# Preparing an LSTM's weights in fewer, larger pieces, half an element apart, in elements 3 to 27

## The chip, the cores and the metric

The kernel runs on one core of one Trainium2 chip. A core has five engines that run side by side, each with its own queue that is worked off in order: TensorE (PE, matrix products, with its weight loads listed as PEld), VectorE (DVE), ScalarE (ACT), GpSimd (POOL) and SyncE (SP), which here does little but issue DMAs. An engine that waits for another waits on a semaphore, and everything behind the waiting instruction in its queue waits with it. The metric is the device time of one execution in microseconds (us); lower is better.

## What is computed

Two layers, each a graph attention followed by a sequence mixer, each added to x, on x of 32 elements x 512 nodes x 256 features with an adjacency of 32 x 512 x 512:

```python
x = x + gnn0(layernorm(x), adj, ...)        # 4 heads, edge type 1
x = x + mamba2(layernorm(x), ...)           # chunked state-space block, 8 heads of 64
x = x + gnn1(layernorm(x), adj, ...)        # 1 head, all edges
x = x + lstm(layernorm(x), ...)             # below

# the LSTM: 32 rows, 512 steps, hidden size 256
x_proj = einsum('btd,gd->btg', x, W_ih) + b_ih + b_hh
gates = x_proj[t] + h @ W_hh.T ; i, f, g, o = split(gates, 4)
c = sigmoid(f) * c + sigmoid(i) * tanh(g) ; h = sigmoid(o) * tanh(c)
logits = lstm_out @ W_lin + b_lin ; w = argmax(logits) * lstm_out
result = 2 * lstm_out + prefix_sum(w) * fw_att + suffix_sum(w) * bw_att
```

The LSTM's weights `W_ih` and `W_hh` (each 256 x 1024 as laid out for the kernel), its biases, and the small vectors `W_lin`, `b_lin`, `fw_att` and `bw_att` don't depend on x. They are brought into the form that the recurrence wants (gates reordered, halved for a tanh-only evaluation, the last input row subtracted from the others) before it starts, and this preparation is what the change moves.

## The kernel before, in words

There are two phases. `layers_per_batch` takes the 32 elements one after the other through everything but the LSTM and stores each result to `X3` in device memory. Then `recurrence` runs 512 steps over all elements at once.

**The order in the first phase.** The work of an element is cut into generators: `plain0` (first attention), `after0` (its norm), `mamba_in` and `mamba_dt` (preparing the mixer), `mamba` (the mixer) and `plain1` with `after1` (second attention, ending with the `X3` store, L878 and L879). Each generator yields a position on a common axis on which 1.0 is one element. Five streams are merged by always running the one with the least position (L1015 to L1018), so that at one time the mixer of element b, the second attention of b - 1 and the first attention of b + 2 run beside each other. That gives the order in which instructions are recorded; a list scheduler then orders each engine's queue before the kernel is built, and semaphores are added where an instruction needs what another engine or a DMA makes.

The end of one element and the start of the next, as it matters here: PE forms the mixer's output `po` (L847) and the sum of its squares `psc` (L859); DVE copies it to `ssc` (L861); POOL makes its reciprocal root, with the helper `rstd_of`: one scaling `ve` (L54) and one power `rs` (L56); DVE adds the scaled output to x (L865). Behind L865 in DVE's queue stand the reductions for the next first attention (L446, L448), whose result ACT needs for `rowsa`, and PE for `pca`. POOL also does the additions of bias vectors: `blin` to x (L605), `beta` to the x of b + 2 (L494), and `bias0` to the first attention's output `o` (L593), which DVE needs for L341.

**The weights.** The fifth stream is `recurrence_weights`. It works in pieces, each of three steps with a yield between: DMAs bring raw weights into an SBUF tile, POOL transforms them, a DMA stores the result to the buffer `wr` in device memory. A piece of `wih` (8 of them: 2 halves k of 128 input rows, 4 quarters q of 256 gate columns) loads `rwraw` and a broadcast row `rwoff`, subtracts (L1132), clears two spare columns of the tile `rwt` (L1069) and does four scalings from `rwraw` into `rwt` (L1075). A piece of `whh` (8 too) loads `rwraw` by four DMAs and has one more scaling, a column from `wl` (L1135). All tiles are of pool `rw0` with one buffer per tag: two tags for `rwraw` (by q), one for `rwoff`, one for `rwt`. So a new `rwt` can't be written until the store of the last one (L1140) has read it. Pieces of `wih` with k = 1 store 127 rows, as their last row is the bias; the others store 128.

`begun` copies one column of the x of the element in progress into a tile ahead of its load, so that the load can't be issued before that element is there. The position of this stream is set in one line (L1014): it starts 1.75 elements before the end and all its steps fall within 1.5 elements. `recurrence` loads `wr` in three DMAs (L1283) when the first phase is done.

Of the kernel before, what the change touches and what calls it, by code (L numbers as in the profile page):

```python
# [14 lines left out]
ALU = mybir.AluOpType  # L15
# [4 lines left out]
P = 128  # L20
N = 512
NT = N // P
D = 256
DK = D // P
# [9 lines left out]
GB = 32  # L34
# [41 lines left out]
def layers_per_batch(ctx, tc, c, a, X3, odd=None, wr=None):  # L76
# [6 lines left out]
    nc = tc.nc  # L83
    nb = a.x.shape[0]
# [917 lines left out]
    def each(*parts):  # L1002
        return stream([(b + at, b + until, make, b + n) for b in range(-2, nb + 1) for at, until, make, n in parts])

    streams = [
        each((0.0, 1.0, mamba, 0)),
        each((-0.097, -0.039, mamba_in, 0), (-0.026, 0.192, mamba_dt, 0)),
        each((0.55, 0.857, second, -1), (0.857, 1.52, first, 2)),
        each((1.62, 1.74, after0, 2)),
    ]  # L1010
    if odd is not None:
        rw = ctx.enter_context(tc.tile_pool(name="rw0", bufs=1))
        now = lambda: states[int(min(at))]["x"][:, 0, 0:1]
        streams.append(nb - 1.75 + 1.5 / 64 * n for n, _ in enumerate(recurrence_weights(nc, rw, a, wr, now)))  # L1014
    END = nb + 10  # L1015
    at = [next(t) for t in streams]
    while min(at) < END:
        n = at.index(min(at))  # L1018
        at[n] = next(streams[n], END)

    if odd is not None:
# [12 lines left out]
        for most, n in ((mall0, H0), (mall1, 1)):  # L1034
            pair = wp.tile([4 * n, n], F32, name=f"pair{n}")
# [12 lines left out]
def recurrence_weights(nc, pool, a, wr, now):  # L1048

    Q, J = 4, 64
    W = 4 * J + 2
    nw = DK * Q * W
    n0 = 2 * nw  # L1060
    half = (0.5, 0.5, 0.5, 1.0)
    order = (3, 1, 0, 2)

    def tile_(p, n, tag):
        return pool.tile([p, n], F32, tag=tag, name=tag)

    def ordered(raw, n, s):
        t = tile_(P, W, "rwt")
        nc.gpsimd.memset(t[:n, 4 * J :], 0.0)  # L1069
        halves = t[:n, : 3 * J].rearrange("p (e g j) -> p e g j", e=2, g=3)  # L1070
        for to, g in enumerate(order):
            dst, src = t[:n, 3 * J : 4 * J], raw[:n, g * J : (g + 1) * J]
            if to < 3:
                dst, src = halves[:, :, to, :], src.rearrange("p (e j) -> p e j", e=2)
            nc.gpsimd.tensor_scalar(dst, src, half[g] * s, None, ALU.mult)  # L1075
        return t

    def begun(t, *columns):
        for n in columns or (0,):
            nc.gpsimd.tensor_copy(t[:, n : n + 1], now())  # L1080
        return t

    yield

    wl = begun(tile_(P, 2 * DK, "rwl"), 0, DK)
    for q in range(Q):
        for l in range(2):
            nc.sync.dma_start(
                out=wl[q * 32 : (q + 1) * 32, l * DK : (l + 1) * DK],
                in_=a.wl[q : q + 1, l * J : (l + 1) * J].rearrange("o (k p) -> p (o k)", p=32),  # L1090
            )
    yield
    nc.gpsimd.tensor_tensor(wl[:, :DK], wl[:, DK:], wl[:, :DK], ALU.subtract)
    bl = begun(tile_(P, 2, "rbl"))
    nc.sync.dma_start(out=bl, in_=a.bl.to_broadcast([P, 2]))
    b = [begun(tile_(P, 4 * J, f"rwraw{n}")) for n in range(2)]
    for t, src in zip(b, (a.bih, a.bhh)):
        nc.sync.dma_start(out=t[:Q], in_=src.rearrange("o (q r) -> (o q) r", q=Q))
    yield
    nc.gpsimd.tensor_tensor(bl[:, 0:1], bl[:, 0:1], bl[:, 1:2], ALU.subtract)  # L1100
    nc.gpsimd.tensor_tensor(b[0][:Q], b[0][:Q], b[1][:Q], ALU.add)
    t = ordered(b[0], Q, 1.0)
    yield
    nc.sync.dma_start(out=wr[:, n0 + 2 * J : n0 + 2 * J + 1], in_=bl[:, 0:1])
    last = wr[P - 1 : P, nw - Q * W : nw].rearrange("o (q w) -> (o q) w", q=Q)
    nc.sync.dma_start(out=last, in_=t[:Q])
    yield
    for n, src in enumerate((a.fw, a.bw)):
        t = begun(tile_(P, W, "rwt"))
        for q in range(Q):  # L1110
            nc.sync.dma_start(out=t[q * GB : (q + 1) * GB, :J], in_=src[q : q + 1, :].to_broadcast([GB, J]))
        yield
        nc.gpsimd.tensor_scalar(t[:, :J], t[:, :J], 0.5, None, ALU.mult)
        yield
        nc.sync.dma_start(out=wr[:, n0 + n * J : n0 + (n + 1) * J], in_=t[:, :J])
        yield
    for n, (src, s) in enumerate(((a.wih, 1.0), (a.whh, 0.5))):
        for k in range(DK):
            for q in range(Q):
                raw = begun(tile_(P, 4 * J, f"rwraw{q % 2}"))  # L1120
                cols = slice(q * 4 * J, (q + 1) * 4 * J)
                if n == 0:
                    nc.sync.dma_start(out=raw, in_=src[k * P : (k + 1) * P, cols])
                    off = begun(tile_(P, 4 * J, "rwoff"))
                    nc.sync.dma_start(out=off, in_=src[D - 1 : D, cols].to_broadcast([P, 4 * J]))
                else:
                    for r in range(Q):
                        r0 = r * J + k * 32
                        nc.sync.dma_start(out=raw[r * 32 : (r + 1) * 32], in_=src[r0 : r0 + 32, cols])
                yield  # L1130
                if n == 0:
                    nc.gpsimd.tensor_tensor(raw, raw, off, ALU.subtract)  # L1132
                t = ordered(raw, P, s)
                if n == 1:
                    nc.gpsimd.tensor_scalar(t[:, 4 * J : 4 * J + 1], wl[:, k : k + 1], 0.5, None, ALU.mult)  # L1135
                yield
                o0 = n * nw + (k * Q + q) * W

                r = P - 1 if n == 0 and k == DK - 1 else P
                nc.sync.dma_start(out=wr[:r, o0 : o0 + W], in_=t[:r])  # L1140
                yield


def recurrence(ctx, tc, c, a, X3, wr, out):
# [247 lines left out]
@with_exitstack  # L1392
def kernel(ctx: ExitStack, tc: tile.TileContext, a, out):
    nc = tc.nc
    nb = a.x.shape[0]
    const = ctx.enter_context(tc.tile_pool(name="const", bufs=1))
    dram = ctx.enter_context(tc.tile_pool(name="dram", bufs=1, space=DRAM))
    c = setup_consts(nc, const)
    X3 = dram.tile([N, nb, D], F32, name="X3")
    wr = dram.tile([P, 2 * DK * 4 * 258 + 2 * 64 + 1], F32, name="wr")  # L1400
    odd = const.tile([1, 1], I32, name="odd")
    with ExitStack() as phase:
        layers_per_batch(phase, tc, c, a, X3, odd, wr)
    general = nc.values_load(odd, min_val=0, max_val=1, skip_runtime_bounds_check_because="it is only compared with 0")
    with tc.If(general > 0):
        with ExitStack() as phase:
            layers_per_batch(phase, tc, c, a, X3)
    with ExitStack() as phase:
        recurrence(phase, tc, c, a, X3, wr, out)
# [70 lines left out]
```

## Time and profile before

| what | value |
|---|---|
| median of 3 runs | 4633.89 us (4614.34 to 4634.27) |
| the profiled execution | 4607.25 us |
| its span | 4605.5 us |
| busy, of the span | PE 85%, DVE 73%, ACT 64%, PEld 53%, POOL 28% |
| from one `ssc` (L861) to the next, elements 0 to 29 | 97.5 to 98.5 us |
| from 29 to 30, and from 30 to 31 | 133.7 and 90.9 us |
| first and last POOL scaling of weights (L1075) | 3026.0 and 3208.6 us |
| first DMA of `wr` into the recurrence | 3294.0 us |
| the rest, to the end | 1311 us, with DVE busy 93% of the time in 3305 to 4530 |

The first phase is a steady loop of 97.8 us for each element, in which PE, ACT, DVE and POOL hand work to each other many times, and its last two elements are of a different length. Durations of single instructions below come from the profiled execution, which is shorter than the median of the runs by 27 us. A column named idle gives the time for which an engine stood still just before an instruction, and what ended it.

### The profile page before, as it was taken

Reading aid. Unit: us, or ns where it says so; the run is one execution under the profiler, and the core shown is the slowest. Engines: PE = TensorE matmul, PEld = TensorE weight load, DVE = VectorE, ACT = ScalarE, POOL = GpSimd, SP = SyncE. Lnnn points to the kernel's source line nnn. Section 1 sums busy time; section 2 is a strip of 40 time slices with the busy share of each in tenths; the row PEclk is TensorE's granted clock in tenths of the full one; section 3 lists DMA queues with packets and bytes.
Section 4 is the critical chain, followed back from the end, with each engine's and each line's share of the span. In section 5 each row is a group of like instructions: output and inputs, shape, how many; then the busy total and the mean of one; then the engine's idle time right before and its main releaser. Section 6 shows DMA issues by size and latency. Waiting matters only on the chain. (4 is left out here: it accounts for less than half of the span.)

```text
span 4605.5 us, 116255 instructions
## 1 busy us (share of the span) xinstructions
PE 3910.5 (85%) x46798; PEld 2447.7 (53%) x46798; DVE 3345.0 (73%) x10429; ACT 2957.3 (64%) x6852; POOL 1275.3 (28%) x1371
## 2 busy tenths in 40 slices
PE   6888899988999888999888999867688888888883
PEld 3445554445554455544455544534466666666662
DVE  4676666676666776666766667745599999999997
ACT  4777777777777777777777777755344444444441
POOL 2333433334333334333334333344000000000000
PEclk8999999999999999999999999988899999999997
DMA  3111222121222212221112221221112222222225
GB/s 109 52 62 57 74 65 72 61 63 57 73 70 67 65 59 65 74 71 61 63 56 74 65 72 60 63 65 57 55 36 45 45 45 45 45 45 44 45 41 167
DMA packets 273755, 288.69 MB, mean 63 GB/s; under 512 B 151872, under 2 KB 224536, under 8 KB 271032
## 3 DMA queue, kind: packets, MB, share of 16 engines
q1 hardware_dynamic: 269832, 271.32, 20.8%
q10 hardware_dynamic: 3216, 9.81, 0.7%
q8 instruction: 371, 6.08, 0.6%
q14 instruction: 176, 1.44, 0.1%
q0 software_dynamic: 160, 0.04, 0.0%
HBM read 227.09 MB, written 37.11 MB: 57 GB/s over the span
## 5 line engine op out<-in xcount | busy, mean ns | idle before, releaser
L1267 PE MATMUL pg<-wall,h 128*32 128x96 f32 x16352 | 558.8, 276 | 176.8 <-DVE h L1349 169.3
L1267 PEld LDWEIGHTS pg<-wall,h 128*32 128x32 f32 x16352 | 374.1, 109 | 350.9 <-DVE h L1349 331.9
L1267 PE MATMUL pg<-wall,xTr 128*32 128x96 f32 (+1 forms) x16384 | 549.0, 274 | 0.0
L484 DVE SCALAR_TENSOR_TENSOR w<-w,adjT 128x1024 f32<-128x1024 f32 x256 | 348.5, 1382 | 249.2 <-ACT w L478 249.2
L1267 PEld LDWEIGHTS pg<-wall,xTr 128*32 128x32 f32 x16384 | 447.3, 110 | 5.0 <-issue 0.3
L710 DVE SCALAR_TENSOR_TENSOR acc<-px,convw,acc 128x511 f32<-128x511 f32 (+2 forms) x480 | 351.3, 744 | 84.6 <-ACT acc L705 76.8
L1326 ACT ACTIVATE z<-pg 128x96 f32<-128x96 f32 x512 | 128.7, 251 | 438.9 <-PE pg L1267 438.9
L478 ACT ACTIVATE w<-rb,neg,colsa 128x512 f32<-128x512 f32 x512 | 387.4, 807 | 8.0 <-PE psu L556 4.4
L746 POOL TENSOR_TENSOR ce<-ce,cT 128x384 f32<-128x384 f32 x128 | 185.2, 1476 | 658.6 <-ACT cT L718 654.9
L548 PE MATMUL pav<-w,hb 128*64 128x512 f32 x1024 | 351.8, 613 | 7.7 <-DVE w L484 4.6
L1337 ACT ACTIVATE z<-z 128x32 f32<-128x32 f32 x1024 | 234.7, 229 | 168.7 <-DVE z L1335 101.0
L829 PE MATMUL py<-g,xdt 128*64 128x128 f32 x2048 | 179.8, 315 | 179.2 <-DVE g L765 131.9
L760 ACT ACTIVATE g<-bc,cs 128x128 f32<-128x128 f32 x1024 | 324.4, 389 | 9.9 <-DMA bc<-line 6.6
L689 PE MATMUL px<-mT,win 128*128 128x512 f32 x640 | 305.1, 608 | 0.0
L54 POOL TENSOR_SCALAR ve<-mv 128x4 f32<-128x4 f32 x32 | 6.2, 194 | 1064.4 <-DVE mv L1191 1064.4
L56 POOL TENSOR_TENSOR rs<-ve,mhalf 128x4 f32<-128x4 f32 (+1 forms) x224 | 276.1, 1233 | 18.4
L847 PE MATMUL po<-wc,xh 128*128 128x256 f32 x1024 | 264.9, 404 | 4.6 <-DVE xh L817 2.5
L829 PEld LDWEIGHTS py<-g,xdt 128*64 128x64 f32 x2048 | 137.7, 157 | 236.3 <-DVE g L765 138.9
L1349 DVE STREAM_TRANSPOSE h<-hh 128x32 f32<-128x32 f32 x1024 | 216.4, 211 | 34.9
L689 PE MATMUL pz<-mT,win 128*128 128x512 f32 x512 | 240.4, 602 | 0.0
L962 PE MATMUL pov<-wb,wv 128*128 128x257 f32 x1024 | 236.5, 384 | 2.0 <-DVE wv L484 2.0
L1332 DVE SCALAR_TENSOR_TENSOR ab<-z 128x64 f32<-128x64 f32 x1024 | 226.7, 221 | 15.1 <-ACT z L1326 11.8
(249 smaller groups left out, 8539.6 us busy)
## 6 DMA issues: line engine op xcount, KB each, us to landing
bc<-line SPq DMA_DIRECT2D x128, 512.0 KB, 3.6
adj<-in_adj_dram SPq DMA_DIRECT2D x32, 1024.0 KB
rb<-linea SPq DMA_DIRECT2D x64, 512.0 KB, 5.0
ce<-line SPq DMA_DIRECT2D x64, 384.0 KB, 4.6
x<-in_x_dram SPq DMA_DIRECT2D x32, 512.0 KB, 6.5
X<-x SPq DMA_DIRECT2D x32, 512.0 KB
xt<-X SPq DMA_DIRECT2D x128, 128.0 KB, 2.1
x<-X SPq DMA_DIRECT2D x128, 128.0 KB, 3.5
```

Source lines behind the costliest of these rows:

```text
L56: nc.gpsimd.tensor_tensor(rs, ve, c.mhalf[:, :n], ALU.pow)
L478: nc.scalar.activation(w[:, t, k, :], rb[:, k, :], AF.Relu, bias=neg1, scale=cols[:, 2 * m + t, h + k : h + k + 1],)
L484: nc.vector.scalar_tensor_tensor(w[:, :, k, :], w[:, :, k, :], 1.0, edges, ALU.add, ALU.mult)
L548: nc.tensor.matmul(pa[k * HO : (k + 1) * HO, :], hb[:, j, 2 * q + k, :], w[:, t, k, :], start=(j == 0), stop=(j == NT - 1),)
L689: nc.tensor.matmul(pz, win[:, k, col : col + P], mT[:, k, :], start=(k == 0), stop=(k == DK - 1))
L710: nc.vector.scalar_tensor_tensor(acc[:, s:], pz[:, : N - s], convw[:, cc, k : k + 1], acc[:, s:], ALU.mult, ALU.add)
L760: nc.scalar.activation(g[:, i, k, :], bc[:, k, i * P : (i + 1) * P], AF.Relu, bias=cs[:, i, 2 * cc + k : 2 * cc + k + 1], scale=-1.0,)
L829: nc.tensor.matmul(py[k * HD : (k + 1) * HD, i * P : (i + 1) * P], xdt[:, i, h * HD : (h + 1) * HD], g[:, i, k, :], start=(i == 0), stop=F ...
L847: nc.tensor.matmul(po[:, i * D : (i + 1) * D], xh[:, cc, it * P : (it + 1) * P], wc[:, cc, :], start=(cc == 0), stop=(cc == NC - 1),)
L962: nc.tensor.matmul(po[:, : D + 1], ws[j // 2][:, j % 2, 0, it * P : (it + 1) * P], wb[:, j, :], start=(j == 0), stop=(j == NT - 1),)
L1267: nc.tensor.matmul(p[q * GB : (q + 1) * GB, :], lhs[k], w[:, k, q, s:e], start=(start and k == 0), stop=(stop and k == DK - 1),)
L1337: nc.scalar.activation(z[:, (10 + n) * H : (11 + n) * H], z2[:, 4 * n * H : (4 * n + 1) * H], AF.Tanh, scale=0.5)
```

## The change

The position of the fifth stream changes: its steps now start at 3.25 and are (32 - 8)/48 = 0.5 elements apart. The work is cut differently:

- `rwraw` and `rwt` have one tag each and are twice as wide. `rwraw` takes raw weights and the broadcast row side by side (in `wih`), or two quarters (in `whh`); `rwt` two quarters.
- `ordered` takes one or two quarters. Three of its four scalings are now two each, of 32 columns for every quarter, so it has seven instead of four.
- `whh` has four pieces of two quarters each instead of eight; `wih` keeps eight of one, in the order q, k instead of k, q.
- `fw` and `bw` share a tile, a scaling and a store; the loads of `wl` come in two steps.

What is computed and stored is the same. The core of the diff:

```diff
-        streams.append(nb - 1.75 + 1.5 / 64 * n for n, _ in enumerate(recurrence_weights(nc, rw, a, wr, now)))
+        streams.append(3.25 + (nb - 8) / 48 * n for n, _ in enumerate(recurrence_weights(nc, rw, a, wr, now)))
...
-    def ordered(raw, n, s):
-        t = tile_(P, W, "rwt")
-        nc.gpsimd.memset(t[:n, 4 * J :], 0.0)
-        halves = t[:n, : 3 * J].rearrange("p (e g j) -> p e g j", e=2, g=3)
+    def ordered(raw, n, quarters, s):
+        t = tile_(P, 2 * W, "rwt")
+        tq = t.rearrange("p (q w) -> p q w", q=2)[:n, :quarters]
+        rq = raw.rearrange("p (q w) -> p q w", q=quarters)[:n]
+        nc.gpsimd.memset(tq[:, :, 4 * J :], 0.0)
         for to, g in enumerate(order):
-            dst, src = t[:n, 3 * J : 4 * J], raw[:n, g * J : (g + 1) * J]
+            src = rq[:, :, g * J : (g + 1) * J]
             if to < 3:
-                dst, src = halves[:, :, to, :], src.rearrange("p (e j) -> p e j", e=2)
-            nc.gpsimd.tensor_scalar(dst, src, half[g] * s, None, ALU.mult)
-        return t
+                for e in range(2):
+                    nc.gpsimd.tensor_scalar(
+                        tq[:, :, (3 * e + to) * 32 : (3 * e + to + 1) * 32], src[:, :, e * 32 : (e + 1) * 32],
+                        half[g] * s, None, ALU.mult,
+                    )
+            else:
+                nc.gpsimd.tensor_scalar(tq[:, :, 3 * J : 4 * J], src, half[g] * s, None, ALU.mult)
+        return t, tq
...
+    t = begun(tile_(P, 2 * W, "rwt"))
     for n, src in enumerate((a.fw, a.bw)):
-        t = begun(tile_(P, W, "rwt"))
         for q in range(Q):
-            nc.sync.dma_start(out=t[q * GB : (q + 1) * GB, :J], in_=src[q : q + 1, :].to_broadcast([GB, J]))
+            nc.sync.dma_start(out=t[q * GB : (q + 1) * GB, n * J : (n + 1) * J], in_=src[q : q + 1, :].to_broadcast([GB, J]))
         yield
-        nc.gpsimd.tensor_scalar(t[:, :J], t[:, :J], 0.5, None, ALU.mult)
-        yield
-        nc.sync.dma_start(out=wr[:, n0 + n * J : n0 + (n + 1) * J], in_=t[:, :J])
-        yield
+    nc.gpsimd.tensor_scalar(t[:, : 2 * J], t[:, : 2 * J], 0.5, None, ALU.mult)
+    yield
+    nc.sync.dma_start(out=wr[:, n0 : n0 + 2 * J], in_=t[:, : 2 * J])
+    yield
...
+    for q in range(Q):
+        cols = slice(q * 4 * J, (q + 1) * 4 * J)
         for k in range(DK):
...
+            pair = begun(tile_(P, 2 * 4 * J, "rwraw"), 0, 4 * J)
+            raw, off = pair[:, : 4 * J], pair[:, 4 * J :]
+            nc.sync.dma_start(out=raw, in_=a.wih[k * P : (k + 1) * P, cols])
+            nc.sync.dma_start(out=off, in_=a.wih[D - 1 : D, cols].to_broadcast([P, 4 * J]))
+            yield
+            nc.gpsimd.tensor_tensor(raw, raw, off, ALU.subtract)
+            t, _ = ordered(raw, P, 1, 1.0)
+            yield
+            o0 = (k * Q + q) * W
+            r = P if k < DK - 1 else P - 1
+            nc.sync.dma_start(out=wr[:r, o0 : o0 + W], in_=t[:r, :W])
+            yield
+    for q in (0, 2):
+        for k in range(DK):
+            raw = begun(tile_(P, 2 * 4 * J, "rwraw"))
+            for r in range(Q):
+                r0 = r * J + k * 32
+                nc.sync.dma_start(out=raw[r * 32 : (r + 1) * 32], in_=a.whh[r0 : r0 + 32, q * 4 * J : (q + 2) * 4 * J])
+            yield
+            t, tq = ordered(raw, P, 2, 0.5)
+            for e in range(2):
+                nc.gpsimd.tensor_scalar(tq[:, e, 4 * J : 4 * J + 1], wl[:, k : k + 1], 0.5, None, ALU.mult)
+            yield
+            o0 = nw + (k * Q + q) * W
+            nc.sync.dma_start(out=wr[:, o0 : o0 + 2 * W], in_=t)
+            yield
```

More of the change, by code (lines that the diff above doesn't have):

```diff
@@ L1085, in recurrence_weights @@
     wl = begun(tile_(P, 2 * DK, "rwl"), 0, DK)
-    for q in range(Q):
-        for l in range(2):
+    for l in range(2):
+        for q in range(Q):
             nc.sync.dma_start(
@@ L1095, in recurrence_weights @@
     nc.sync.dma_start(out=bl, in_=a.bl.to_broadcast([P, 2]))
-    b = [begun(tile_(P, 4 * J, f"rwraw{n}")) for n in range(2)]
+    both = begun(tile_(P, 2 * 4 * J, "rwraw"), 0, 4 * J)
+    b = [both[:, : 4 * J], both[:, 4 * J :]]
     for t, src in zip(b, (a.bih, a.bhh)):
@@ L1101, in recurrence_weights @@
     nc.gpsimd.tensor_tensor(b[0][:Q], b[0][:Q], b[1][:Q], ALU.add)
-    t = ordered(b[0], Q, 1.0)
+    t, _ = ordered(b[0], Q, 1, 1.0)
     yield
@@ L1105, in recurrence_weights @@
     last = wr[P - 1 : P, nw - Q * W : nw].rearrange("o (q w) -> (o q) w", q=Q)
-    nc.sync.dma_start(out=last, in_=t[:Q])
+    nc.sync.dma_start(out=last, in_=t[:Q, :W])
     yield
+    t = begun(tile_(P, 2 * W, "rwt"))
     for n, src in enumerate((a.fw, a.bw)):
-        t = begun(tile_(P, W, "rwt"))
         for q in range(Q):
-            nc.sync.dma_start(out=t[q * GB : (q + 1) * GB, :J], in_=src[q : q + 1, :].to_broadcast([GB, J]))
+            nc.sync.dma_start(out=t[q * GB : (q + 1) * GB, n * J : (n + 1) * J], in_=src[q : q + 1, :].to_broadcast([GB, J]))
@@ L1112, in recurrence_weights @@
         yield
-        nc.gpsimd.tensor_scalar(t[:, :J], t[:, :J], 0.5, None, ALU.mult)
-        yield
-        nc.sync.dma_start(out=wr[:, n0 + n * J : n0 + (n + 1) * J], in_=t[:, :J])
-        yield
-    for n, (src, s) in enumerate(((a.wih, 1.0), (a.whh, 0.5))):
-        for k in range(DK):
[L1119 to L1141, printed above, removed]
@@ new lines, in recurrence_weights @@
+    nc.gpsimd.tensor_scalar(t[:, : 2 * J], t[:, : 2 * J], 0.5, None, ALU.mult)
+    yield
+    nc.sync.dma_start(out=wr[:, n0 : n0 + 2 * J], in_=t[:, : 2 * J])
+    yield
+    for q in range(Q):
+        cols = slice(q * 4 * J, (q + 1) * 4 * J)
+        for k in range(DK):
+            pair = begun(tile_(P, 2 * 4 * J, "rwraw"), 0, 4 * J)
[10 more added lines that the diff above has]
+            yield
@@ new lines, in recurrence_weights @@
+    for q in (0, 2):
[11 more added lines that the diff above has]
+            nc.sync.dma_start(out=wr[:, o0 : o0 + 2 * W], in_=t)
+            yield
```

## The prediction

> **What bounds the kernel now.** I read the page first. Its chain of work that ended last starts only at the recurrence (3291 us to the end), which the change does not touch, so the 3290 us before it must be read by stage. The table of windows compares one steady element, 1640.5 to 1738.3, with elements 30 and 31, each counted from its first `zs` (L697). Columns: us, then busy us of PE, PEld, DVE, ACT, POOL, then granted clock, DMA share, GB/s.
>
> ```profile
> 1640.50:1738.30 97.80, 87.61 (x432) 49.49 (x431) 66.55 (x140) 73.26 (x131) 36.89 (x33) 0.97 0.22 65
> 3031.30:3168.60 137.30, 92.91 (x401) 48.33 (x400) 66.83 (x137) 66.64 (x119) 53.30 (x92) 0.84 0.20 55
> 3168.60:3250.10 81.50, 57.22 (x275) 35.62 (x275) 37.16 (x66) 46.10 (x85) 25.91 (x66) 0.87 0.24 70
> ```
>
> Element 30 has the work of any other and takes 137.3 us instead of 97.8. The waits of 3105 to 3220 (engine, line, releaser: total, times, longest) say why:
>
> ```profile
> DVE o L341 <- POOL o L593: 30.8, 1, 30.8
> POOL rwt L1069 <- DMA wr<-rwt: 27.9, 8, 8.2
> ACT dec L670 <- DMA wr<-rwt: 7.1, 1, 7.1
> ACT g L760 <- DMA bc<-line: 6.6, 2, 4.8
> ```
>
> DVE waits 30.8 us for a bias addition on POOL, and POOL is late because weight pieces stand ahead of it, each waiting until the previous one has left the only `rwt` buffer. The timelines of POOL and SP (start, us, what, idle before and its releaser) show two prices for that wait:
>
> ```profile
> 3087.70 0.25 SPq L1140 DMA_DIRECT2D wr<-rwt  x1
> 3095.85 0.10 POOL L1069 MEMSET rwt<- 128x2 f32 x1 [8.05 <-DMA wr<-rwt]
> 3106.53 0.10 POOL L1069 MEMSET rwt<- 128x2 f32 x1 [8.19 <-DMA wr<-rwt]
> 3106.59 2.48 POOL L593 TENSOR_TENSOR o<-o,bias 128x512 f32<-128x512 f32 x2
> ...
> 3174.83 0.34 SPq L1140 DMA_DIRECT2D wr<-rwt  x1
> 3176.68 0.10 POOL L1069 MEMSET rwt<- 128x2 f32 x1 [1.75 <-DMA wr<-rwt]
> ```
>
> A store of 128 rows frees the buffer 1.85 us after its issue (3174.83 to 3176.68); one of the four with 127 rows takes 8.15 us (3087.70 to 3095.85; the other three 8.1 to 8.2).
>
> Last, a steady element where the moved work will stand, timelines of POOL and DVE:
>
> ```profile
> 1646.57 2.49 POOL L494 TENSOR_TENSOR x<-x,beta 128x512 f32<-128x512 f32 x2
> 1649.02 1.27 POOL L605 TENSOR_TENSOR x<-x,blin 128x512 f32<-128x512 f32 x1
> 1652.61 0.20 POOL L54 TENSOR_SCALAR ve<-ssc 128x4 f32<-128x4 f32 x1 [2.32 <-DVE ssc L861]
> 1652.89 1.02 POOL L56 TENSOR_TENSOR rs<-ve,mhalf 128x4 f32<-128x4 f32 x1
> ...
> 1652.36 0.16 DVE L861 COPY ssc<-psc 128x4 f32<-128x4 f32 x1 [6.88 <-PE psc L859]
> 1653.94 0.48 DVE L865 SCALAR_TENSOR_TENSOR x<-po,rs,x 128x256 f32<-128x256 f32 x1 [1.42 <-POOL rs L56]
> 1654.46 0.68 DVE L446 TENSOR_REDUCE mall<-pra 16x1 f32<-16x512 f32 x1
> ```
>
> POOL has 2.32 us free before L54. But L54 is on the loop that sets the 97.8 us: followed back step by step from one L861 to the one before, each instruction starts within 0.2 us of what releases it: psc (PE), L861, POOL L54 and L56, DVE L865, L446 and the queue behind them as far as `da` (L650), then PE. While POOL is late there, DVE stands at L865, and behind it L446 and L448; ACT's `rowsa` and PE's `pca` (1656.47) wait for those.
>
> **What the Trainium skill says.** "DMA: Bandwidth & Descriptors", section "Why a DMA increments its semaphore by 16 and not by 1", says that the number of engines is the largest up to 16 that divides the slowest dimension, so 128 rows use 16 and 127 rows one. The trace agrees: 127 packets of 1032 B follow one another over 6.7 us, 128 of them are done in 0.5. "TensorE: Matmul & The Clock Gate", section "What's actually happening", has PE fall to half clock after an idle window of about 3.4 us. The trace agrees: 0.50 is granted in 1635.3 to 1642, behind a 4.1 us wait of PE, and in 3109.5 to 3116.5, after the long stall.
>
> **The change, part by part.** The compiled order of the changed kernel keeps every other instruction of SP, POOL, DVE, ACT and PE in its place up to the work of element 31, apart from the moved work.
>
> (1) Elements 30 and 31 lose the work: the gain. Element 30 needs 97.8 at most; three things differ at its end. Its L861 came 125.2 us after its first `zs`, against 88.9 in a steady element; without first(32), whose transposes and `pra` interleave with `po`, I take 86.5. From L861 to the next first `zs` it took 12.2; a `rs` held up by 2 us behind a weight piece goes, leaving 10.2. So 96.7 for 137.3: 40.6 gained. In element 31 three stalls go: ACT's 7.1 (its `line` store waited for the slot of a weight DMA; 6.8 of it passes on), 1.8 and 4.8 for `bc`, which SP issued late behind weight DMAs: 13.4. Together 54. At least 47 (the stalls of 31 half hidden), at most 62 (ACT's new order there helps as well). The last 33.4 us, from L865 of element 31 to the last `X`, stay.
>
> (2) Eight wih pieces, all in one place, at the ends of elements 6 to 17. SP issues `raw` and `off` after the adj load, on POOL's copies, at about 1646.9 and 1647.3 in the element above. `off` was used 3.1 to 3.3 us after issue in the tail, so 1650.5. POOL's second L605 ends at 1650.7 (0.36 later, for two copies). Then the subtraction 0.73 and gap 0.1, six scalings of 128x32 (64 columns start every 0.33, one column every 0.14 to 0.17, so about 0.245) 1.47, and one of 64 columns 0.37: end at 1653.35, 0.75 after L54 is due. That alone would be small. But the next piece's memset stands right behind, **ahead of L54**, and waits until this piece's store has left the buffer; with one `rwt` the stall that cost most before comes along.
>  - 128 rows (k = 0): store at 1653.4, memset at 1655.5 (1.85, and 0.25 for traffic), L54 at 1655.6: 3.0 late. Bounds 2.0 and 4.5.
>  - 127 rows (k = 1): store at 1653.4, memset at 1661.55, L54 at 1661.65: 9.0 late. Bounds 8.3 and 11.
>
>  Four of each: 12 + 36 = 48. Nothing hides it, as L54 is on the loop.
>
> (3) PE idles meanwhile from 1656.45 and comes back at half clock. After the long stall of element 30, the stretch from the first xdt (L783) to the last `came` (L812) took 10.0 us for a steady 7.7: 2.3. I take 2.3 for each 9 us stall and 1.2 for each 3 us one: 14. Bounds 0 and 20.
>
> (4) Four whh pieces, at the ends of elements 18 to 23, stand behind L56 of L54's pair. Six scalings of 64 columns 2.0 and one of 128 about 0.5 from 1653.9 end at 1656.4; store of twice the bytes 2.4, memset and two one-column scalings 0.6: the next L54 (1658.40) starts at 1659.6, 1.2 late. Three times, since no memset follows the last: 3.6. Bounds 0 and 10.
>
> (5) The beginning: bias block about 0.6; the eight `wl` loads hold SP 4 us, so x lands near 1655, and its statistics start at 1658.2: nothing. fw and bw: one scaling of 0.5 ends before 1652.6: nothing, and its memset falls in the 4.5 us before the next L54. The last wih piece carries 0.5 more. Together 1.1.
>
> (6) Moved past on SP: `X` out goes 2.3 us later (nobody waits), the x load behind the store's wait 5 us later, landing by 1658 (k = 0) or behind the slow store by 1664, where its statistics start at 1661 or 1667: nothing, with 3 us to spare.
>
> Sum: −54 + 48 + 14 + 3.6 + 1.1 = +13 us. The profiled execution took 4607.25 (span 4605.5), so 4620. The median shown is 4633.89, 27 above it; 13 on top gives 4647. About 23 us, 0.5%, is what a measurement of this kernel can tell from no change.
>
> **Rivals.**
> A, the stalls come to more. In the 127-row pieces the store's engine also carries x rows, and PE's lost clock adds where PE is the tight one; or element 31 keeps its stalls. At 13 us for each k = 1 piece and 7 for each k = 0, 80 is lost with (4) and (5) at 5 more; against 54 that is +31, 4665. It decides once the eight pieces cost 73 together, the mean then over 9. For it: nothing is free behind L54. Against: store and load times are measured.
> B, faster: the stall is absorbed. Were the store or the loop looser than I read it (another buffer of the pool given to the next `rwt`, or stages that make up half of it), 20 would be lost and 54 gained: −34, 4600. It decides below 31 us lost. For it: POOL is busy 28% overall. Against: no gap over 0.2 us on that loop, and the memset's wait stands in the compiled order.
> C, the change does not do what it says, the tail keeping its stalls: excluded for POOL and SP, since nothing of it is left there; that 30 and 31 shrink by under 35 for another reason gives +32 and goes with A.
>
> **How the numbers follow.** My case has 52 in 100, A with C 36, B 12. The gain's 47 to 62 and the losses' ends (piece stalls 41 to 62, clock 0 to 20, whh 0 to 10) span −20 to +46 if all ends fall together. A leans upward, so I keep the upper end and take −16 to +46 for 8 in 10: 4618 to 4680. Faster by over 0.5%: B, 0.12. Within: 0.52. Slower: 0.36.
>
> **What would show it.** From one L861 to the next: about 95 us from element 29 to 30 instead of 133.7, and about 76 from 30 to 31 instead of 90.9; behind elements 6 to 17, alternately about 102 and 109, with 97.8 between; the wait of memset `rwt` for `wr<-rwt` still some 40 us, and POOL's `rs` as what DVE L865 waits for. Part (2) is wrong if L54 starts within 1 us of L861 there, part (3) if the granted clock stays 1 behind the stalls, part (1) if DVE still waits on L593 by tens of us.

## The result, and the profile after

The changed kernel takes 4638.9 us (median of 20 runs, 4621.0 to 4646.2); the kernel before, run beside it, 4618.7 us (20 runs, 4603.7 to 4639.3). The ratio is 1.0031, with a 95% interval of 1.0016 to 1.0045: about 14 us slower (7 to 21), which on the 4633.9 us shown before is 4648. It is not the quotient of the medians, which lie 20 us apart: the runs of before fall into two groups, eleven from 4604 to 4619 us and nine from 4633 to 4639, and their median is at the edge of the lower one. The means, 4637.4 and 4623.2, differ by 14. The profiled executions differ by more, 4605.5 to 4634.8 us of span, in large part because a steady element takes 97.9 us on average in the one of before, and 98.9 in many elements without a piece in that of the changed kernel. Both lengths come without any difference of work (last section).

First the windows, for the same columns as before: an element that follows a piece of 127 rows (from its L861 to the next), one that follows a piece of 128 rows, one without a piece, and then elements 30 and 31, each from its first `zs`.

```profile
976.40:1085.20 108.80, 90.08 (x430) 50.38 (x431) 66.58 (x140) 73.15 (x130) 39.77 (x44) 0.92 0.20 63
1085.20:1187.70 102.50, 89.96 (x431) 50.38 (x430) 66.58 (x140) 73.17 (x130) 38.19 (x38) 0.95 0.23 69
1187.70:1286.60 98.90, 88.74 (x431) 49.34 (x431) 66.51 (x140) 73.24 (x130) 37.60 (x35) 0.97 0.20 62
...
3112.10:3213.20 101.10, 88.23 (x402) 47.39 (x400) 65.51 (x137) 67.10 (x122) 30.89 (x28) 0.97 0.13 42
3213.20:3280.70 67.50, 54.53 (x276) 35.21 (x275) 37.36 (x65) 45.31 (x83) 12.89 (x12) 0.94 0.18 56
```

DVE, ACT and POOL are as busy in the first three windows as in any other element; the extra 10 and 4 us are waiting. Elements 30 and 31 went from 137.3 and 81.5 to 101.1 and 67.5: the tail's gain is there, and the loop has given it back, and more.

Where, the waits over the whole span show (total, times, longest), first of before, then of after:

```profile
POOL rwt L1069 <- DMA wr<-rwt: 48.7, 13, 8.2
DVE x L865 <- POOL rs L56: 44.0, 31, 1.4
```

```profile
DVE x L865 <- POOL rs L56: 99.1, 32, 11.7
POOL rwt L1072 <- DMA wr<-rwt: 50.0, 12, 8.3
```

POOL waits for its own stores as long as before, 50 us. What changed is who stands behind it: DVE's wait for `rs` at L865, 1.4 us in every element before, has grown by 55 us. One piece of each kind in the timelines of POOL, SP and DVE of the changed kernel:

```profile
977.24 0.37 POOL L1082 TENSOR_SCALAR rwt<-rwraw 128x64 f32<-128x64 f32 x1
985.82 0.10 POOL L1072 MEMSET rwt<- 128x2 f32 x1 [8.22 <-DMA wr<-rwt]
986.00 0.20 POOL L54 TENSOR_SCALAR ve<-ssc 128x4 f32<-128x4 f32 x1
...
977.63 0.25 SPq L1140 DMA_DIRECT2D wr<-rwt  x1
977.98 1.09 SPq L108 DMA_DIRECT2D x<-in_x_dram  x1
...
976.41 0.16 DVE L861 COPY ssc<-psc 128x4 f32<-128x4 f32 x1 [6.61 <-PE psc L859]
987.35 0.48 DVE L865 SCALAR_TENSOR_TENSOR x<-po,rs,x 128x256 f32<-128x256 f32 x1 [10.78 <-POOL rs L56]
...
1709.67 0.10 POOL L1072 MEMSET rwt<- 128x2 f32 x1 [2.08 <-DMA wr<-rwt]
```

The scalings are done at 977.61, 1.2 us after `ssc`. Then the memset for the next piece, an element or more away, waits 8.22 us for the store of this one, and L54 behind it comes 9.6 us after L861; behind the 128-row piece (1709.67) the wait is 2.08.

From one L861 to the next: 102.5 to 102.6 us behind the four pieces of 128 rows, 108.8 to 109.5 behind the four of 127, and 98.4 to 99.2 in nearly all others up to element 22. From element 0 to 29 that is 2921.2 us against 2838.3 before (+82.9), from 29 to 31 174.3 against 224.6 (-50.3).

### The profile page after: what moved, and what is told of

Its sections match the earlier page's. It is cut to its first block, busy times and chain, and to the rows that moved or that the text cites. A ratio compares the mean times of both kernels' runs of the same rounds, so it can differ in the third digit from the quotient of the medians.

```text
span 4634.8 us, 116234 instructions
## 1 busy us (share of the span) xinstructions
PE 3936.6 (85%) x46798; PEld 2457.6 (53%) x46798; DVE 3345.3 (72%) x10429; ACT 2954.4 (64%) x6852; POOL 1276.3 (28%) x1384
## 5 line engine op out<-in xcount | busy, mean ns | idle before, releaser
L484 DVE SCALAR_TENSOR_TENSOR w<-w,adjT 128x1024 f32<-128x1024 f32 x256 | 347.8, 1379 | 248.1 <-ACT w L478 248.1
L710 DVE SCALAR_TENSOR_TENSOR acc<-px,convw,acc 128x511 f32<-128x511 f32 (+2 forms) x480 | 351.5, 743 | 75.6 <-ACT acc L705 67.8
L746 POOL TENSOR_TENSOR ce<-ce,cT 128x384 f32<-128x384 f32 x128 | 185.1, 1475 | 696.0 <-ACT cT L718 679.0
L829 PE MATMUL py<-g,xdt 128*64 128x128 f32 x2048 | 167.9, 299 | 178.8 <-DVE g L765 131.7
L54 POOL TENSOR_SCALAR ve<-mv 128x4 f32<-128x4 f32 x32 | 6.2, 193 | 1063.9 <-DVE mv L1205 1063.9
L829 PEld LDWEIGHTS py<-g,xdt 128*64 128x64 f32 x2048 | 125.8, 145 | 240.8 <-DVE g L765 138.9
L689 PE MATMUL pz<-mT,win 128*128 128x512 f32 x512 | 253.1, 629 | 0.0
```

The costliest lines, as they stand in the source:

```text
L484: nc.vector.scalar_tensor_tensor(w[:, :, k, :], w[:, :, k, :], 1.0, edges, ALU.add, ALU.mult)
L689: nc.tensor.matmul(pz, win[:, k, col : col + P], mT[:, k, :], start=(k == 0), stop=(k == DK - 1))
L710: nc.vector.scalar_tensor_tensor(acc[:, s:], pz[:, : N - s], convw[:, cc, k : k + 1], acc[:, s:], ALU.mult, ALU.add)
L829: nc.tensor.matmul(py[k * HD : (k + 1) * HD, i * P : (i + 1) * P], xdt[:, i, h * HD : (h + 1) * HD], g[:, i, k, :], start=(i == 0), stop=F ...
```

## The experiments

The claims to test: the loss is the memset's wait for the store, at the one place where L54 stands behind it (rival: the block of scalings and its loads); and the tail's loss was the same wait. All ratios are to before, with 95% intervals; the three columns on the right come from the profiles, L861 to L861. Each is one execution, and the two lengths of a steady element alone can move the column 0 to 29 by up to 32 us.

| kernel | median us | ratio | element 0 to 29 | 29 to 30 | 30 to 31 |
|---|---|---|---|---|---|
| before | | 1 | 2838.3 | 133.7 | 90.9 |
| changed | 4638.9 | 1.0031 (1.0016 to 1.0045) | 2921.2 | 100.1 | 74.2 |
| e1_halves | 4631.8 | 1.0028 (1.0012 to 1.0044) | 2915.8 | 99.9 | 75.5 |
| e2_split127 | 4604.9 | 0.9991 (0.9970 to 1.0011) | 2888.6 | 98.7 | 74.2 |
| e3_place | 4575.3 | 0.9909 (0.9878 to 0.9941) | 2857.8 | 99.8 | 75.6 |
| e4_before_split | 4597.2 | 0.9962 (0.9942 to 0.9983) | 2857.4 | 118.3 | 85.1 |
| e5_none | 4589.1 | 0.9917 (0.9888 to 0.9947) | 2838.0 | 100.4 | 73.9 |
| e6_late | 4616.7 | 0.9983 (0.9961 to 1.0004) | 2869.2 | 117.2 | 93.5 |
| e7_two_tiles | 4648.0 | 1.0055 (1.0035 to 1.0075) | 2929.8 | 99.9 | 77.9 |
| e9_place_split | 4555.3 | 0.9888 (0.9843 to 0.9933) | 2838.3 | 100.1 | 74.1 |
| e10_one_memset | 4608.5 | 0.9976 (0.9958 to 0.9995) | 2891.7 | 99.8 | 75.6 |
| e11_spread | 4629.5 | 1.0031 (1.0013 to 1.0049) | 2915.6 | 99.9 | 77.9 |
| e12_both | 4580.9 | 0.9919 (0.9892 to 0.9946) | 2864.5 | 98.7 | 74.2 |

**A second place for the result (e1, e7).** Two ways to give the memset a buffer that is free:

```diff
-            t, _ = ordered(raw, P, 1, 1.0)
+            t, _ = ordered(raw, P, 1, 1.0, pairt[:, k * W : (k + 1) * W])   # e1: halves of one tile
...
-        t = tile_(P, 2 * W, "rwt")
+        t = tile_(P, W, f"rwt{h}")                                         # e7: h = k for wih
```

> The changed kernel with one thing undone: pieces of wih with k = 0 use the left half of the buffer rwt and those with k = 1 the right half, so that the memset that stands ahead of L54 (ve<-ssc) no longer waits for the store just issued. Size, loads, scalings and their places stay. My theory (the wait of the memset is the price): L54 starts about 1 us after L861 behind the pieces instead of 3.5 and 9.9; only the last piece, behind which a memset of the whole buffer stands, still costs some 9. Gain against the changed kernel 4 x 2.5 + 3 x 8.9 = 37 us and up to 10 of lost TensorE clock; against before a ratio of 0.990 to 0.996. Rival (the block itself, its loads or its traffic delay L54): L54 still over 3 us late and the ratio at 1.000 or above.

> The changed kernel with two separate tiles of one quarter each, rwt0 for k = 0 and rwt1 for k = 1, in place of one of two quarters; whh pieces fill both and store them with two DMAs (fourteen scalings for seven, some 1.3 us more in each of four pieces). In seven of the eight wih pieces the memset ahead of L54 then waits for a store of an element or two ago; only behind the last one it still waits for the store just issued. My theory (the wait is the price): L54 starts 1 to 1.5 us after L861 behind the first seven pieces and some 10 behind the last; 4 x 2.4 + 3 x 8.8 = 36 us gained, 5 lost in whh, 31 in all against the changed kernel, ratio against before 0.993 to 0.998. Rival (halves e1 changed nothing since the block itself is the price): L54 late as in the changed kernel and the ratio at 1.001 or above.

Both expectations fail. The memset waits 47.6 us for stores in either kernel, and L54 comes as late as in the changed kernel behind all eight pieces but one of e1. This is not the rival's doing. In the traces the memset stands as early as its data allow: with two buffers the one for the piece after next has come forward too, to just behind the last piece that used its half, and waits for that piece's store as before (it starts 8.1 to 8.2 us after the issue of each 127-row store of e1). One piece of e1 tells the two apart by accident. It has no memset behind it (the next one clears both halves, and must wait for the other):

```profile
1709.33 0.37 POOL L1082 TENSOR_SCALAR rwt<-rwraw 128x64 f32<-128x64 f32 x1
1709.78 0.20 POOL L54 TENSOR_SCALAR ve<-ssc 128x4 f32<-128x4 f32 x1
```

There L54 came 1.29 us after L861: the block alone costs 1.0 us (a steady L54 comes after 0.25). The ratio of e7 is above that of the changed kernel, though the intervals overlap; its longer whh pieces, of fourteen scalings and two stores, go with three elements of 100.4 to 103.9 us.

**The number of rows (e2).**

```diff
-            nc.sync.dma_start(out=wr[:r, o0 : o0 + W], in_=t[:r, :W])
+            for r0, r1 in ((0, r),) if r == P else ((0, 112), (112, r)):
+                nc.sync.dma_start(out=wr[r0:r1, o0 : o0 + W], in_=t[r0:r1, :W])
```

> The changed kernel with the store of 127 rows issued as two, of 112 and of 15 rows, and nothing else. My theory (k = 1 pieces cost three times as much as k = 0 pieces because one DMA engine carries all their 127 rows): L54 starts 3.5 to 4 us after L861 in k = 1 pieces too, instead of 9.9; 4 x 6.2 = 25 us and up to 4 of clock gained against the changed kernel; ratio against before 0.995 to 0.999. Rival (k = 1 pieces are slow for their place or the traffic of x at that time): under 5 us gained, ratio 1.002 or above.

The waits of e2 over the span:

```profile
DVE x L865 <- POOL rs L56: 75.7, 32, 5.6
POOL rwt L1072 <- DMA wr<-rwt: 25.9, 12, 2.4
```

As expected: the longest wait falls from 8.3 to 2.4, L54 comes 3.6 to 4.0 us after L861 behind these pieces too, and their elements take 101.7 to 102.6 us for 108.8 to 109.5. The ratio falls from 1.0031 to 0.9991, just above the range that I expected. The row count is the cause of the difference between the two kinds of piece.

**The memset itself (e10).**

```diff
+    rwt = tile_(P, 2 * W, "rwt")
+    nc.gpsimd.memset(rwt, 0.0)
...
-        nc.gpsimd.memset(tq[:, :, 4 * J :], 0.0)
```

> The changed kernel with one tile rwt for all pieces, whose spare columns are cleared once at the start instead of by a memset in each piece. Still one buffer; but the first instruction of the next piece that writes it is now a scaling, which stands behind that piece's load, an element or two later. The memset was placed as early as its buffer allowed, right behind the last piece that had used it, which is why halves (e1) and two tiles (e7) left its wait where it was. My theory (that wait is the price, not the block): L54 starts about 1.3 us after L861 behind seven pieces, as behind the one piece of e1 that had no memset behind it; behind the last one, where a column of wl takes the memset's place, it still starts about 10 after. Gain 4 x 2.3 + 3 x 8.5 = 35 us against the changed kernel; ratio against before 0.993 to 0.998. Rival (the block of a piece is the price): as the changed kernel, 1.001 or above.

L54 comes as expected: 0.3 to 2.1 us after L861 behind seven pieces, 9.6 behind the last. So the wait is what held it up. The ratio lies in the range too. But three elements behind 127-row pieces still take 105.2 to 106.6 us, although their L54 is about 1 us late. The timelines of SP and DVE, and then the waits over the span, show for e10 what the stall had covered:

```profile
973.38 0.25 SPq L1142 DMA_DIRECT2D wr<-rwt  x1
973.72 1.11 SPq L108 DMA_DIRECT2D x<-in_x_dram  x1
...
983.02 0.43 DVE L65 BATCH_NORM_STATS2 bnst<-x 128x6 f32<-128x256 f32 x1 [3.86 <-DMA x<-in_x_dram]
```

```profile
DVE x L865 <- POOL rs L56: 62.8, 32, 10.8
POOL rwt L1153 <- DMA wr<-rwt: 15.6, 4, 8.3
DVE bnst L65 <- DMA x<-in_x_dram: 15.3, 4, 3.9
```

The load of the next x is issued 0.34 us behind the 127-row store and lands 9.3 us after its issue. DVE waits at L65, and behind L65 stand `ee` (L635) and what leads to `da`. (One wait of 3.7 is at the kernel's start, in every kernel here; three of 3.9 are new.)

**Both (e12).** e10 with e2's split.

> e10 (spare columns cleared once) and the 127-row stores issued as two, of 112 and 15 rows. In e10 L54 came only 0.9 to 1.3 us after L861 behind pieces of k = 1, but these elements still took 105.2 to 106.6 us, and DVE L65 waited 3.9 us for the x load, which SP issues 0.3 us behind the slow store. My theory now (the one-engine store has a second price, the x load that shares its engine; the memset's wait covered it): no wait of L65 for x, k = 1 elements at 98.5 to 100 us but for the last, about 102; 18 to 20 us less than e10, ratio against before 0.989 to 0.996. Rival (something else holds k = 1 elements, such as TensorE's clock after the piece): they stay over 104 us and the ratio within 0.002 of e10's 0.9976.

The waits of e12 over the span:

```profile
DVE x L865 <- POOL rs L56: 58.4, 32, 4.9
DVE bnst L65 <- DMA x<-in_x_dram: 3.7, 1, 3.7
```

No wait of L65 for x is left but that at the start, and the elements behind 127-row pieces take 98.8 to 99.7 us, the last one 102.7. In the first of them L65 reads the x 4.8 us after its issue and need not wait, against 9.3 us with the wait in e10. From 0 to 29 it is 27 us less than e10, where I had expected 18 to 20: 20 us in the three elements whose L65 waited, 6 in the last one, where the wait for the buffer is shorter too (400.8 for 426.8 in the four). The ratio goes from 0.9976 to 0.9919. A 127-row store therefore has two prices, the wait for the buffer and the x load behind it; how it holds that load back is not shown. In the changed kernel the first hides the second.

**The place (e3, e9), and the floor (e5).**

```diff
-        now = lambda: states[int(min(at))]["x"][:, 0, 0:1]
+        now = lambda: da[:, 0, 0:1]
```

> The changed kernel with one thing changed: the column that begun copies ahead of a load comes from da (L650, mid-element) and not from x. The same pieces with the same single buffer and the same waits then stand behind the last statistics of an element on POOL, ahead of L746, where POOL is free for over 20 us. My theory (the same wait costs nothing where nothing on the loop is queued behind it): the memsets of rwt still wait some 40 to 50 us for stores, but L54 (ve<-ssc) starts 0.25 us after L861 in every element; 55 us or more gained against the changed kernel, ratio against before 0.986 to 0.992. Rival (the work costs the loop time wherever it stands, by its traffic, by sharing POOL and DVE, or by the TensorE clock): ratio 0.998 or above, and elements with a piece longer than those without.

> e3_place (begun copies a column of da) and the 127-row stores issued as two, of 112 and 15 rows. My theory (in that place a wait of 8 us has nothing queued behind it that is needed): the waits of memset rwt fall from 52 to some 26 us and the time does not move, ratio within 0.002 of e3's 0.991. Rival (a slow store still costs by its engine or by what it delays on SP): 0.988 or below.

> The preparation of the weights is left out: the buffer wr is filled with zeros by nine DMAs in elements 3 to 8, so the LSTM computes with zero weights; everything else is the changed kernel's. This is the floor for any place of the work. My theory (in e3 the work costs nothing where it stands): within 0.002 of e3's 0.991. Rival (it still costs by traffic or sharing): below 0.988. For the lengths of elements: if stretches of 98.9 to 99.0 us for an element instead of 97.5 to 98.4 come here too, they have nothing to do with the weights.

e5 leaves the preparation out: nine DMAs fill `wr` with zeros in elements 3 to 8, and the LSTM computes with zero weights. The waits of e3 over the span, and its POOL timeline at a 127-row piece:

```profile
POOL rwt L1072 <- DMA wr<-rwt: 51.7, 12, 8.3
DVE x L865 <- POOL rs L56: 45.4, 32, 1.4
```

```profile
998.20 0.10 POOL L1072 MEMSET rwt<- 128x2 f32 x1 [8.27 <-DMA wr<-rwt]
1001.86 5.60 POOL L746 TENSOR_TENSOR ce<-ce,cT 128x384 f32<-128x384 f32 x4 [3.56 <-DMA ce<-line]
```

The same pieces with the same single buffer wait 51.7 us, even longer than in the changed kernel, and L865 no longer feels it: 45.4, its 1.4 us in each element. L54 comes 0.25 us after L861 everywhere. Behind the memset POOL waits another 3.6 us for L746's own data. The ratio, 0.9909, is as I expected. e9 halves the memset's waits (27.1); its 0.9888, of six runs, lies between my range and the rival's, and the intervals don't tell it from e3's. Without the preparation (e5) the ratio is 0.9917, as expected, and element 0 to 29 takes 2838.0 us against 2838.3 with it in e9. In that place no cost of the work can be seen, and e3 and e9 beat both kernels by 0.9 to 1.4%.

**The parts alone (e4, e6, e11).** e4 is before with only the split of e2; e6 has the changed kernel's pieces at the position of before; e11 has before's pieces at the changed position:

```diff
-        streams.append(3.25 + (nb - 8) / 48 * n for ...      # changed
+        streams.append(nb - 1.75 + 1.5 / 48 * n for ...      # e6
...
-        streams.append(nb - 1.75 + 1.5 / 64 * n for ...      # before
+        streams.append(3.25 + (nb - 8) / 64 * n for ...      # e11
```

> The kernel before with its four stores of 127 rows issued as two each, of 112 and of 15 rows, and nothing else. My theory of the tail (element 30 is 40 us too long since L593 stands behind weight pieces, three of which wait 8.2 us for a 127-row store): these waits fall to about 2 us each; element 30 gets 15 to 25 us shorter, ratio 0.994 to 0.997. Rival (the number of pieces or their loads set element 30's length): element 30 as before, ratio within 0.002 of 1.

> The changed kernel's pieces at the position of before (1.75 elements before the end, all within 1.5 elements): one part of the change alone, the size. My theory (the tail's cost is the waits for the stores, and the four 127-row stores stay): 29 to 30 stays over 120 us, ratio 0.996 to 1.003. Rival (larger pieces are the gain by themselves): ratio below 0.994.

> The kernel before with its own sixteen small pieces, at the changed kernel's place: steps from 3.25, (32 - 8)/64 = 0.375 apart. This is the other part of the change alone, the spreading. My theory (the loss is the memset's wait on the loop, the gain the emptied tail; the size does neither): L54 3 to 4 us late behind four pieces of wih and some 9.8 behind four, nothing behind pieces of whh; 29 to 30 about 100 us; ratio against before 1.000 to 1.005, as the changed kernel's. Rival (fewer and larger pieces are needed for the spreading to pay): 1.008 or above, with whh pieces that delay the loop too.

The waits of e4 in its elements 30 and 31 (3040 to 3260 us):

```profile
POOL rwt L1069 <- DMA wr<-rwt: 24.1, 13, 3.2
DVE o L341 <- POOL o L593: 14.4, 1, 14.4
```

As expected, 29 to 30 falls by 15.4 us by the split alone, from 133.7 to 118.3, as L341's wait for L593 falls from 30.8 to 14.4; 30 to 31 goes from 90.9 to 85.1. So about 21 of the tail's 50 us were the price of the 127-row stores. In e6 29 to 30 is 117.2 (I had written over 120), 30 to 31 is 93.5: larger pieces in the old place shorten the one and not the other, and the interval of the whole holds 1. e11 comes out at the changed kernel's 1.0031, with L54 2.8 to 3.1 us late behind four pieces and 8.7 to 9.3 behind four; pieces of whh delay it by 0.3 to 1.2, which I had put at nothing. So the size of the pieces hardly matters to the loss; the spreading makes it.

## Why the prediction was right

The forecast was 4647 with 13 us lost; measured is 1.0031, 14 us. The mechanism was right: the tail's stalls go, and the memset's wait costs the loop about as much at L54. That the two numbers agree to 1 us is luck. The interval alone is 7 to 21 us; steps 1 and 2 below were 8 us too good together, which step 3 made up with 2 to 11 us too much; and 4633.9, the base, is the median of three runs of which two were of the longer group, while the profile it was joined to is of the shorter. Step by step, against the profile:

1. Tail: 54 expected, 50.3 measured. Element 31 gave 14.0 for 13.4. Element 30 gave 36.2 for 40.6, and the term that was off is the 86.5 us to its L861: I had taken 2.4 off a steady element for the missing first(32), but it took 91.6, and 91.8 with no weights anywhere (e5). From there to the next `zs` 9.5 for 10.2. That "L861 29 to 30" would be about 95 came from the same term; it is 100.1.
2. The eight wih pieces: 48 expected. L54 was late by 3.2 to 3.6 (expected 3.0) and 9.3 to 10.3 (expected 9.0), 13.3 + 38.8 = 52.1 in all. The mechanism is shown by e2, e10 and e3: the rows set its size, the memset carries it, the place decides whether it counts. The "Trainium skill", page "DMA: Bandwidth & Descriptors", section "Why a DMA increments its semaphore by 16 and not by 1", gave the row rule, and 8.2 against 2.2 us for 127 rows and 112 + 15 (e2) agrees.
3. Half clock after the stalls: 14 expected. The clock does fall: 0.50 is granted for 13.7 us behind each 127-row piece and for 6.8 behind each of 128 rows, 0.92 and 0.95 in the mean of the windows above. But its price could not be separated. The loop's 82.9 us less 52.1, the 1.5 by which the bias piece held up L54 and the 4.3 below leave 25 us: 13 of them in the 19 elements that have no piece, many of 98.9 us, and 12 in the eight. e3 has 17 elements of 99.0 us or more without any stall of L54. Measured against 98.9 the eight elements exceed it by 55.5 us, which leaves 3.4 for the clock; against 97.9 it would be between 11 and 12. Step 3 was right in size only if one counts the second way, and the prediction did not know of the two lengths.
4. whh: 3.6 expected, as three times 1.2. The first statistics' L54 was 1.1 late in three elements, 18, 20 and 21. But only one of them, 20, is longer, 103.2 us, 4.3 above the next, with 6.8 us of half clock from 17.7 us behind its L861; 18 and 21 took 98.6 and 98.9. So the sum came near for another reason than the one given, and why 20 alone is longer stays open.
5. Beginning: 1.1 expected, the bias piece alone held up L54 by 1.5.
6. SP: right, as L65 finds the loaded x at 992.52 without a wait, 14.5 us after its issue; with the 9.3 us to landing of e10 some 5 us were to spare, for 3 expected. But I did not say what they hang on. The start at 1667 in the prediction has the stall of step 2 in it, and a steady one is at 1658.2, before the slow landing at 1664. e10 took the stall away: 3.9 us of waiting, and elements some 7 us longer.

Rival A needed a mean of over 9 us for a piece; it was 6.5 by the lateness of L54, and 6.9 to 7.9 by the length of the elements. The profiles' own balance, 82.9 lost and 50.3 gained, is 32.6 us and looks like its +31, but 13 us of it lie in elements without a piece, and no stall explains them. B needed the stall absorbed; DVE's wait at L865 grew by as much as POOL was late. The way in which B imagined it, another buffer for the next `rwt`, was tried (e1, e7) and would have changed nothing.

## What to carry to other kernels

A wait costs what is queued behind it: before moving work into a gap, look at the last instruction that it issues, not only at its length. A scheduler that pulls instructions forward to the earliest place their data allow will put a trivial one (a memset of two columns) in front of the loop with a wait for a store, and more buffers only move it with them; clear such columns once, or tie the work to data that appear where the engine has time. When a stall is removed, look for the transfer that it had covered.

## What the runs showed of the hardware

**Two lengths of an element, and the clock's windows.** In e4 nothing differs from before until element 29. Its windows (same columns): three elements in a row, one later, and the stretches of granted clock in one of each kind.

```profile
1065.00:1163.30 98.30, 88.14 (x430) 49.84 (x431) 66.52 (x140) 73.19 (x130) 36.82 (x32) 0.97 0.21 65
1163.30:1260.80 97.50, 87.16 (x430) 48.79 (x431) 66.52 (x140) 73.20 (x130) 36.83 (x32) 0.98 0.22 66
1260.80:1358.50 97.70, 87.55 (x430) 49.44 (x431) 66.50 (x140) 73.23 (x130) 36.80 (x32) 0.97 0.21 66
1457.70:1556.70 99.00, 88.82 (x430) 49.39 (x431) 66.55 (x141) 73.18 (x130) 36.83 (x32) 0.97 0.21 65
...
1146.80:1153.70 6.90, 5.93 (x29) 5.07 (x30) 5.81 (x18) 6.06 (x10) 5.61 (x6) 0.51 0.48 145
1416.50:1419.90 3.40, 3.40 (x5) 1.19 (x4) 2.83 (x7) 1.41 (x3) 1.19 (x2) 0.50 0.01 4
1443.80:1447.20 3.40, 3.40 (x16) 2.80 (x13) 2.56 (x10) 2.56 (x7) 3.22 (x4) 0.50 0.48 123
```

Up to element 12 one stretch of half clock comes in each element, of 3.4 or 6.9 us, and three elements take 293.5; from then on two of 3.4 come, and every element takes 99.0. The "Trainium skill", page "TensorE: Matmul & The Clock Gate", section "What's actually happening", says that the clock is set in free-running windows of 3413 ns. 99.0 is 29 of them, and 293.5 is 86. The stretches of half clock in these traces last 3.41 us or a multiple of it. So the loop seems to settle into step with the windows in two ways, 1.1 us per element or 32 us per run apart. That fits the runs of before in the experiments' rounds, most of which lie near 4601 or near 4634 us; that the windows cause it is argued, not shown. The weights don't: in e4 and e6 the long elements come while every piece still lies ahead, and e5, without the preparation, has runs near 4553 and near 4590 us. In e1 and e10 the switch followed a 1.2 us delay in element 3. It is why 0.5% was hard to tell here.

**POOL copies beside DVE.** In e3 the two copies of one column into `rwraw` take 1.1 and 1.2 us here, and 0.18 each in the changed kernel; DVE starts `w` (L484, two operands in SBUF) just ahead of them. POOL and DVE timelines:

```profile
981.23 2.25 POOL L1087 COPY rwraw<-da 128x1 f32<-128x1 f32 x2 [4.14 <-DVE da L650]
...
981.09 2.35 DVE L484 SCALAR_TENSOR_TENSOR w<-w,adjT 128x1024 f32<-128x1024 f32 x2
```

The "Trainium skill", page "SBUF — State Buffer", section "SBUF: two separate sides", describes ports that DVE and GpSimd share as an exclusive lock for a whole instruction; two instructions of 1.2 us on DVE, and two copies that each end within 0.05 us of one of them, agree with it.
